# Householder reflections beside two attentions: three long steps each, or six short ones

## Chip, cores and metric

The kernel runs on one core of a Trainium2 chip. The metric is the device time of one execution in microseconds (us). "Before" is the kernel without the change, "after" the kernel with it. Engines are named as in the profile: PE is TensorE, DVE is VectorE, ACT is ScalarE, POOL is GpSimd, SP is SyncE, which here only issues DMAs.

## The reference

The activations x have the shape (4, 512, 288) and pass through four layers. L0 is an attention with adaptive layer norm and a mixture of four experts, of which two serve each token. L1 and L3 are attentions with adaptive layer norm and a dense two-layer MLP. L2 is a rotation in a 64-dimensional subspace that depends on a weight P (288 x 64) and on the condition, but not on x:

```python
U, _ = jnp.linalg.qr(P)                       # 288 x 64
R = _rotation(cond, W, b)                     # expm of a skew 64 x 64 matrix
z = jnp.einsum('btn,nd->btd', x, U)
z_rot = jnp.einsum('btd,bde->bte', z, R)
x_rot = x + jnp.einsum('btd,nd->btn', z_rot - z, U)
```

The attentions have 16 heads of 18 features and 512 positions for each of the four batches; all arithmetic is float32.

## The kernel before

**Order of the layers.** One program runs L0's attention (`attention(0, ...)`), the experts of L0, L1's attention, L1's MLP, the rotation's products, L3's attention and L3's MLP, one behind the other. Nearly all of the time belongs to matmuls on PE.

**The work that runs beside.** The subspace U of L2 depends on weights alone, so the kernel computes it beside the layers ahead of L2. `rotation()` (L839) is a Python generator: `reflections()` (L584) makes the QR of P by 64 Householder reflections, one after the other, on the transposed matrix `pT` (64 rows on partitions, 288 columns, and two more columns for the head and the factor of the reflection at hand). Then `subspace()` turns the reflections into U. Each `yield` ends a step. `tick()` (L863) advances the first generator of the list `beside` by one step, and the places where tick() is called decide between which other instructions a step's instructions are issued. At first the list holds only `rotation()`; in round 4 of L0's attention the rest of L0's modulation is put ahead of it for a short while (L1234), and L3's modulation is appended behind it.

**One reflection k, before the change, is three steps:**
- *The long step.* `reflect` (L572) applies reflection k - 1 to the rows that are left: `headed` (L553) copies the head (L554), `dots` (L557) multiplies rows and v and sums (L560, which the profile shows as a product and an accumulator read), L577 makes the factor `w2`, and L578 updates `pT`. Then the norm of the next row: `dots` again, `n2` (L611) and `sgn` (L612), all on DVE, and the square root as a power on POOL (`nrm`, L613).
- *The short step.* Six small DVE operations (L618 to L623: `sn`, head, `den`, its maximum, reciprocal, factor `c`), and then `reflector` (L546) issues on SP a DMA (L550) that spreads the row of `pT` over the partitions of the tile `v`.
- *An idle step*, in which nothing is issued, so that the DMA can land. In the experts' phase, where the flag `far` is set, there are two such steps.

The flag `inside` (L861) is true while an attention issues its quads. Two helpers fix the order within an engine: `beside_of("DVE", ...)` ties an instruction behind the last row maximum issued so far (`take`, L98), and the scheduler may move an instruction that is not tied as its data allow. In the long step the head's copy and the norm's dot are tied to that maximum, in the short step `sn` is.

**The attention.** There are 16 rounds, one for each batch and group of four heads. A round has eight *quads*, k = 0 to 7. A quad (L980) issues two score matmuls for the row maxima of round r and two transposed score matmuls of lagging work, alternating; each lands in a PSUM bank. DVE takes the row maximum of the first kind (`row_max`, L954, the reduction is L965), ACT the exponential of the second kind (`weight`, L967, L977). The four banks are few, so a quad's matmuls wait until the DVE maximum and the ACT exponential of the quads before have freed them. Behind each quad other work is issued (L1237 to L1245): queries and keys, values (their additions on DVE are L917), the sums with the probabilities (`sums`, L990), projections, layer norms. At the end of a round, behind quad 7, `shift` (L1005) turns the maxima over on PE and subtracts them on DVE (L1019), which the next round's lagging matmuls need; this is called the round's border below. Rounds begin with round 0 before the loop of L1230; its border is behind its last quad.

**Where the ticks stand.** In the loop over the quads, L1252 to L1254:

```python
some = ticks if r < feed.sorts_from else ticks // 2
if k % 2 and (k + 3) % (gaps // some) == 0:
    tick()
```

`gaps` is 8. L0's attention has ticks = 4, so a step stands behind quads 1, 3, 5 and 7; from round 10 on (`sorts_from` of the experts, whose sorting takes DVE time there) only behind quads 1 and 5. L1's attention has ticks = 2: behind quads 1 and 5 in all rounds. L3's attention has nothing left to run beside it. The last loop (L1259 to L1271) issues the lagging quads of the last round, with one tick in each place where `k % (NT // ticks)` is 0.

**Other users of SP's queue.** During L0's attention SP issues the copies of the experts' weights (`w1c`, L1586) and a few others, in program order with the DMAs of v.

Of the kernel before, what the change touches and what calls it, by code (L numbers as in the profile page):

```python
# [46 lines left out]
def kernel(ctx: ExitStack, tc: tile.TileContext, a: dict, out: bass.AP):  # L47
# [21 lines left out]
    def bank(tag, name):  # L69
        return psum.tile([P, 512], F32, tag=tag, name=name, bufs=banks[tag])  # L70
# [30 lines left out]
    def beside_of(engine, instruction):  # L101
        if engine in taken:
            ordered(instruction.ins, taken[engine])

    def in_turn(engine, instruction):

        beside_of(engine, instruction)
        take(engine, instruction)
# [427 lines left out]
    pT = cst.tile([RK, C + 2], F32, tag="pT", name="pT")  # L536
# [9 lines left out]
    def reflector(n, k):  # L546

        v = bgp.tile([RK, C + 2], F32, tag="v", name=f"{n}_{k}", bufs=4)
        r = RK - 1 - k
        nc.sync.dma_start(v[0:r, 0 : C + 2 - k], spread(pT[r : r + 1, k : C + 2], r))  # L550
        return v

    def headed(k, v, n):  # L553
        beside_of("DVE", nc.vector.tensor_copy(v[0:n, 0:1], v[0:n, C - k : C - k + 1]))  # L554
        return v[0:n, C - k + 1 : C - k + 2]

    def dots(k, m, v, n):  # L557
        junk = bgp.tile([RK, C], F32, tag="junk", name=f"junk_{k}", bufs=1)
        w = small.tile([RK, 1], F32, tag="w", name=f"w_{k}")
        ins = nc.vector.tensor_tensor_reduce(  # L560
            out=junk[0:n, 0 : m.shape[1]],
            in0=m,
            in1=v,
            scale=1.0,
            scalar=0.0,
            op0=ALU.mult,
            op1=ALU.add,
            accum_out=w[0:n],
        )
        return w[0:n], ins  # L570

    def reflect(k, m, v, n):  # L572

        c = headed(k, v, n)
        w, _ = dots(k, m[0:n, k:C], v[0:n, 0 : C - k], n)
        w2 = small.tile([RK, 1], F32, tag="w2", name=f"w2_{k}")
        nc.vector.scalar_tensor_tensor(w2[0:n], w, -1.0, c, ALU.mult, ALU.mult)  # L577
        nc.vector.scalar_tensor_tensor(  # L578
            m[0:n, k:C], v[0:n, 0 : C - k], w2[0:n], m[0:n, k:C], ALU.mult, ALU.add
        )  # L580
# [3 lines left out]
    def reflections():  # L584

        nc.gpsimd.memset(back, 0.0)
        nc.gpsimd.affine_select(
            out=back,
            in_=back,
            compare_op=ALU.not_equal,  # L590
            fill=1.0,
            base=1 - RK,
            pattern=[[1, RK]],
            channel_multiplier=1,
        )
        ps = bank("de", "psback")
        nc.tensor.matmul(ps[0:RK, 0:C], lhsT=back, rhs=pT[:, 0:C], start=True, stop=True)
        nc.vector.tensor_copy(pT[:, 0:C], ps[0:RK, 0:C])
        for k in range(RK):
            n = RK - k  # L600

            def one(name):
                return small.tile([RK, 1], F32, tag=name, name=f"{name}_{k}")[0:n]


            alpha, tail = pT[0:n, k : k + 1], pT[0:n, k + 1 : C]
            hd, c = pT[0:n, C : C + 1], pT[0:n, C + 1 : C + 2]
            n2, nrm, sgn = one("n2"), one("nrm"), one("sgn")
            rest, ins = dots(k, tail, tail, n)
            beside_of("DVE", ins)  # L610
            nc.vector.scalar_tensor_tensor(n2, alpha, alpha, rest, ALU.mult, ALU.add)  # L611
            nc.vector.tensor_scalar(sgn, alpha, 0.0, 2.0, ALU.is_ge, ALU.mult)  # L612
            in_turn("POOL", nc.gpsimd.tensor_tensor(nrm, n2, phalf[0:n], ALU.pow))  # L613
            yield


            sn, den, rden = one("sn"), one("den"), one("rden")
            beside_of("DVE", nc.vector.scalar_tensor_tensor(sn, sgn, -1.0, nrm, ALU.add, ALU.mult))  # L618
            nc.vector.tensor_add(hd, alpha, sn)
            nc.vector.tensor_mul(den, sn, hd)  # L620
            nc.vector.tensor_scalar_max(den, den, TINY)
            nc.vector.reciprocal(rden, den)
            nc.vector.scalar_tensor_tensor(c, rest, 0.0, rden, ALU.is_gt, ALU.mult)  # L623
            if n > 1:
                v = reflector("v", k)
                yield
                yield
                if far[0]:
                    yield
                reflect(k, pT, v, n - 1)  # L630

    def subspace():

# [205 lines left out]
    def rotation():  # L839
        yield from reflections()  # L840
        yield from subspace()
        for b in range(B):
            ps = bank("de", f"psue_{b}")
            for kc in range(KC):
                nc.tensor.matmul(
                    ps[0:CP, kc * RK : (kc + 1) * RK],
                    lhsT=uT[halves[b // HB], kc * CP : (kc + 1) * CP],
                    rhs=ef[halves[b // HB], b % HB, :],
                    start=True,
                    stop=True,  # L850
                )
            nc.vector.tensor_copy(
                ue[:, b, :, :],
                ps[0:CP, 0 : KC * RK].rearrange("p (k j) -> p k j", j=RK),
            )
            yield

    beside, aside = [rotation()], [exponential()]  # L860
    inside, far = [False], [False]  # L861

    def tick(works=beside):  # L863
        while works and next(works[0], works) is works:
            works.pop(0)


    def attention(l, w, mod, eps, feed, ticks, hT=None, then=None, also=()):

# [10 lines left out]
        with ExitStack() as es:  # L880
# [99 lines left out]
            def quad(halves):  # L980

                for k in range(2):
                    for what, r, n in halves:
                        t, i = n // 2, n % 2 * 2 + k
                        if what is row_max:
                            row_max(r, t, i)
                        else:
                            ps[r, t, i] = weight(r, t, i)
# [133 lines left out]
            def lagging(k):  # L1122

                return [(weight, k // (2 * NT), k % (2 * NT))] if k >= 0 and k < n * 2 * NT else []
# [59 lines left out]
            def work_off(jobs, pieces):  # L1184
                for one in pieces:
                    if one in jobs:
                        next(jobs[one], None)
# [22 lines left out]
            n, gaps = len(groups), 2 * NT  # L1210

            def started(jobs):

                for kind, job in jobs.items():
                    if kind != "R":
                        next(job)
# [13 lines left out]
            for r in range(1, n):  # L1230
                jobs, pieces, steps = others(r)
                started(jobs)
                if r == NG and then is not None:
                    beside.insert(0, then)  # L1234
                for k in range(gaps):
                    quad([(row_max, r, k)] + lagging(8 * r + k - 9))
                    for step in steps[k]:  # L1237
                        step()
                    if k == 1 and r > 1:
                        sums(r - 2, 2)  # L1240
                        sums(r - 2, 3)
                    if k == 5:
                        sums(r - 1, 0)
                        sums(r - 1, 1)
                    work_off(jobs, pieces.get(k, ""))  # L1245
                    if k == gaps - 1:
                        for kind, job in jobs.items():
                            if kind != "R":
                                drain(job)
                        shift(r)  # L1250

                    some = ticks if r < feed.sorts_from else ticks // 2  # L1252
                    if k % 2 and (k + 3) % (gaps // some) == 0:
                        tick()  # L1254

            jobs, _, steps = others(n)
            jobs["A"] = feed.activations()
            started(jobs)
            for k in range(NT + 1):  # L1259
                quad(lagging(8 * n + 2 * k - 9) + lagging(8 * n + 2 * k - 8))  # L1260
                if k < NT:
                    for step in steps[2 * k] + steps[2 * k + 1]:
                        step()
                work_off(jobs, feed.last_pieces[k])
                if k == 0:
                    sums(n - 2, 2)
                    sums(n - 2, 3)
                if k in (2, 3):
                    sums(n - 1, k - 2)
                if k < NT and k % (NT // ticks) == 0:  # L1270
                    tick()  # L1271
            inside[0] = False
            hidden = feed.first(places_of_first())
            next(hidden)
# [14 lines left out]
    def drain(work):  # L1289
        for _ in work:  # L1290
            pass
# [1023 lines left out]
    turning = rotate()  # L2315
# [114 lines left out]
```

## Time and profile before

| what | us |
|---|---|
| three timed executions | 1946.29, 1946.56, 1951.55 (median 1946.56) |
| the profiled execution, its own time | 1953.08 |
| its span, first to last instruction | 1951.4 |
| L0's attention, rounds 1 to 15 | about 47 to 400 of the span |
| L1's attention, rounds 1 to 15 | about 882 to 1204 |
| L3's attention, rounds 1 to 15 | about 1451 to 1769 |
| copies of v before the update (L554), first and last | 71.0 and 1311.2 |
| POOL's power (L613), 64 of them, busy | 35.9 |

In the rows of the profile a line gives the source line, engine, operation, output and inputs with their shapes and the count, then busy time and mean duration of one, then the idle time that the engine had just before these instructions, and what ended it ("<-PE a0s L79" is the matmul that filled tile a0s). Tiles of L0's, L1's and L3's attention begin with a0, a1 and a3; "m" is the tile of the maxima's scores, "s" that of the exponentials'. A matmul stands as two rows of the hardware, so the 256 maxima go with 512 matmul rows. In timelines the columns are start, duration, engine, line, operation, tiles and count, and in brackets the idle time ahead. PEclk gives the clock that PE was granted in 40 slices of the span.

### The profile page before, as it was taken

To read this page: it belongs to the slowest core of one execution; us is meant where nothing else is said; L and a number is where in the kernel's file an instruction comes from. 1 tells how busy PE (TensorE), PEld (TensorE's weight loads), DVE (VectorE), ACT (ScalarE), POOL (GpSimd) and SP (SyncE) were. 2 spreads that over 40 slices of the span, in tenths; PEclk is the share of its full clock that TensorE was granted. 3 is DMA by queue.
4 is the path that set the end of the run, shared out by engine and by line. 5 is a ranking of instruction groups with operands and counts; after the bars stand their busy time and mean duration, and the time that the engine had idled before them with its cause. 6 is when DMAs were issued, how large, how long until landed. Compare 5 with 4: busy or idle time off the path is not lost. (4 is left out here: it accounts for less than half of the span.)

```text
span 1951.4 us, 27946 instructions
## 1 busy us (share of the span) xinstructions
PE 1879.7 (96%) x10385; PEld 997.6 (51%) x10385; DVE 1014.7 (52%) x2836; ACT 740.8 (38%) x1375; POOL 542.9 (28%) x795
## 2 busy tenths in 40 slices
PE   7999999999999999999999999999999999999998
PEld 4434443446777677774344433555554444433565
DVE  4667777734423343447766667162355666564201
ACT  1544454443222122224555455231225555455220
POOL 3021321235344347622322123112401121212101
PEclk9989999889999999999999999999999999999999
DMA  7411122326686457621211111300000111111000
GB/s 148 100 36 39 20 57 54 85 56 195 173 238 201 144 178 221 199 85 31 45 32 28 30 32 19 76 9 5 22 1 14 36 37 23 28 27 23 18 16 25
DMA packets 86986, 136.91 MB, mean 70 GB/s; under 512 B 32292, under 2 KB 67663, under 8 KB 86851
## 3 DMA queue, kind: packets, MB, share of 16 engines
q1 hardware_dynamic: 63554, 61.46, 14.0%
q0 software_dynamic: 23184, 73.66, 12.9%
q8 instruction: 82, 1.34, 0.3%
q14 instruction: 54, 0.43, 0.1%
q10 hardware_dynamic: 112, 0.01, 0.0%
HBM read 103.25 MB, written 20.08 MB: 63 GB/s over the span
## 5 line engine op out<-in xcount | busy, mean ns | idle before, releaser
L965 DVE TENSOR_REDUCE max<-a3m 128x1 f32<-128x512 f32 x256 | 164.7, 686 | 126.5 <-PE a3s L79 117.5
L965 DVE TENSOR_REDUCE max<-a0m 128x1 f32<-128x512 f32 x256 | 165.2, 684 | 91.1 <-PE a0s L79 79.4
L965 DVE TENSOR_REDUCE max<-a1m 128x1 f32<-128x512 f32 x256 | 164.5, 684 | 90.7 <-PE a1s L79 84.6
L977 ACT ACTIVATE a0p<-a0s 128x512 f32<-128x512 f32 x256 | 141.1, 596 | 158.0 <-PE a0s L79 157.7
L977 ACT ACTIVATE a1p<-a1s 128x512 f32<-128x512 f32 x256 | 140.2, 596 | 138.8 <-PE a1s L79 138.8
L977 ACT ACTIVATE a3p<-a3s 128x512 f32<-128x512 f32 x256 | 140.0, 596 | 135.8 <-PE a3s L79 135.7
L79 PE MATMUL a0m<-a0qk,a0qk 32*128 32x512 f32 x512 | 167.0, 659 | 9.0 <-DVE max L965 7.8
L79 PE MATMUL e0h<-e0hT,e0w 128*128 128x256 f32 (+1 forms) x918 | 168.4, 393 | 1.6 <-ACT e0hT L2019 0.9
L79 PE MATMUL e0o<-e0w,e0hm 128*128 128x288 f32 x648 | 167.0, 411 | 2.0 <-ACT e0hT L2019 1.9
L79 PE MATMUL a0s<-a0qk,a0qk 32*128 32x512 f32 x512 | 168.3, 665 | 0.0
L79 PE MATMUL a1m<-a1qk,a1qk 32*128 32x512 f32 x512 | 151.9, 640 | 7.4 <-DVE max L965 6.2
L79 PE MATMUL a3m<-a3qk,a3qk 32*128 32x512 f32 x512 | 150.2, 640 | 6.8 <-DVE max L965 5.5
L613 POOL TENSOR_TENSOR nrm<-n,phalf 64x1 f32<-64x1 f32 (+31 forms) x64 | 35.9, 560 | 429.3 <-DVE n L611 429.1
L79 PE MATMUL a1s<-a1qk,a1qk 32*128 32x512 f32 x512 | 153.3, 639 | 0.2 <-DVE v L554 0.2
L79 PE MATMUL a3s<-a3qk,a3qk 32*128 32x512 f32 x512 | 151.6, 639 | 0.2 <-DVE a3qk L1019 0.2
L79 PEld LDWEIGHTS e0h<-e0hT,e0w 128*128 128x128 f32 (+1 forms) x918 | 128.5, 189 | 34.4 <-issue 14.6
L79 PEld LDWEIGHTS e0o<-e0w,e0hm 128*128 128x128 f32 x648 | 120.0, 190 | 37.0 <-ACT e0hT L2019 5.1
L1399 ACT ACTIVATE e0hm<-e0h,e0w 128x256 f32<-128x256 f32 x144 | 60.5, 470 | 124.5 <-PE e0h L79 123.4
L79 PEld LDWEIGHTS a0m<-a0qk,a0qk 32*128 32x128 f32 x512 | 49.2, 187 | 76.0 <-DVE max L965 41.9
L79 PE MATMUL f1h<-f1hT,w 128*128 128x512 f32 (+1 forms) x216 | 81.3, 616 | 0.4 <-ACT f1hT L509 0.4
L79 PE MATMUL f3h<-f3hT,w 128*128 128x512 f32 (+1 forms) x216 | 79.4, 613 | 0.4 <-ACT f3hT L509 0.4
L79 PEld LDWEIGHTS a1m<-a1qk,a1qk 32*128 32x128 f32 x512 | 44.3, 182 | 69.2 <-DVE max L965 48.4
(524 smaller groups left out, 3152.6 us busy)
## 6 DMA issues: line engine op xcount, KB each, us to landing
eo<-e0r SPq DMA_DIRECT2D x50, 144.0 KB
ada<-in_ada SPq DMA_DIRECT2D x18, 324.0 KB
wr<-in_wrot SPq DMA_DIRECT2D x16, 288.0 KB
xm<-e0m SPq DMA_DIRECT2D x6, 768.0 KB
g<-gates SPq DMA_DIRECT2D x24, 144.0 KB
w<-in_w SPq DMA_DIRECT2D x6, 432.0 KB
x<-in_x SPq DMA_DIRECT2D x16, 144.0 KB
w1c<-in_w SPq DMA_DIRECT2D x8, 288.0 KB
```

Of the source, the lines that this page charges most:

```text
L79: ins = nc.tensor.matmul(*args, **kwargs).ins
L613: in_turn("POOL", nc.gpsimd.tensor_tensor(nrm, n2, phalf[0:n], ALU.pow))
L965: take("DVE", nc.vector.tensor_reduce(m[:, t, i, D : D + 1], ps, AX.X, ALU.max))
L977: take("ACT", nc.scalar.activation(p, ps, AF.Exp, scale=D**-0.5))
L1399: nc.scalar.activation(self.hms[i][f], ps[r], func, bias=b1(f)),
```

## The change

Inside an attention a reflection becomes six steps, and the steps come twice as often. `reflect` becomes a generator with a `yield` ahead of the update of `pT`, and another follows behind the update, ahead of the norm of the next row; both hold only while `inside` is true. The idle steps become two there. In the six steps of a reflection are, in this order: the norm with POOL's power; the short step with the DMA of v; nothing; nothing; copy, dot and `w2` of the application; the update.

A new helper `tick_turning` gives a step to the rotation alone, when it is first in the list. In L0's attention it stands behind the even quads of rounds 1 to 9, so every quad has a step there; from round 10 on, and in L1's attention, it stands behind quads 3 and 7, so every second quad has one. In the last loop it follows every tick. L0's modulation, when it is ahead of the rotation, keeps its old places.

```diff
+    def between():
+        if inside[0]:
+            yield
+
     def reflect(k, m, v, n):
         c = headed(k, v, n)
         w, _ = dots(k, m[0:n, k:C], v[0:n, 0 : C - k], n)
         w2 = small.tile([RK, 1], F32, tag="w2", name=f"w2_{k}")
         nc.vector.scalar_tensor_tensor(w2[0:n], w, -1.0, c, ALU.mult, ALU.mult)
+        yield from between()
         nc.vector.scalar_tensor_tensor(
             m[0:n, k:C], v[0:n, 0 : C - k], w2[0:n], m[0:n, k:C], ALU.mult, ALU.add
         )
...
                 yield
                 yield
-                if far[0]:
+                if far[0] or inside[0]:
                     yield
-                reflect(k, pT, v, n - 1)
+                yield from reflect(k, pT, v, n - 1)
+                yield from between()
...
-    beside, aside = [rotation()], [exponential()]
+    turning = rotation()
+    beside, aside = [turning], [exponential()]
...
+    def tick_turning():
+        if beside and beside[0] is turning:
+            tick()
...
                     if k % 2 and (k + 3) % (gaps // some) == 0:
                         tick()
+                    elif (k + 3) % (gaps // some) == gaps // some // 2:
+                        tick_turning()
...
                 if k < NT and k % (NT // ticks) == 0:
                     tick()
+                    tick_turning()
             inside[0] = False
```

## Prediction

> **What bounds the kernel now.** First the page: busy times, the granted clock, the groups.
>
> ```profile
> PE 1879.7 (96%) x10385; PEld 997.6 (51%) x10385; DVE 1014.7 (52%) x2836; ACT 740.8 (38%) x1375; POOL 542.9 (28%) x795
> ...
> PEclk9989999889999999999999999999999999999999
> ...
> L79 PE MATMUL a0m<-a0qk,a0qk 32*128 32x512 f32 x512 | 167.0, 659 | 9.0 <-DVE max L965 7.8
> ...
> L79 PE MATMUL a1m<-a1qk,a1qk 32*128 32x512 f32 x512 | 151.9, 640 | 7.4 <-DVE max L965 6.2
> L79 PE MATMUL a3m<-a3qk,a3qk 32*128 32x512 f32 x512 | 150.2, 640 | 6.8 <-DVE max L965 5.5
> ```
>
> TensorE sets the end: 96% of the span. VectorE is half idle, so taking work off it is worth nothing by itself; what counts is where TensorE waits for VectorE. The score matmuls do: 9.0 us idle before them in L0's attention (a0), 7.4 in L1's (a1), 6.8 in L3's (a3). L3's attention holds no reflection, so it is the yardstick for what reflections cost.
>
> Idle time understates it: when the maxima come late, the four matmuls of a quad go out in two pairs, which the records count as busy. So I read the TensorE timeline from one quad's first matmul to the next one's, with half of any half-clock time taken off, and set each quad of a0 and a1 beside the same quad of a3 ("r.k" is round r, quad k). One example, the VectorE timeline and then the TensorE timeline:
>
> ```profile
> 102.36 1.29 DVE L965 TENSOR_REDUCE max<-a0m 128x1 f32<-128x512 f32 x2 [1.27 <-PE a0s L79]
> 103.57 0.14 DVE L554 COPY v<-v 61x1 f32<-61x1 f32 x1
> ...
> 104.42 0.51 DVE L578 SCALAR_TENSOR_TENSOR pT<-v,w,pT 61x286 f32<-61x286 f32 x1
> 104.96 0.45 DVE L560 CUSTOM_DVE_ANT_0 junk<-pT 61x284 f32<-61x284 f32 x1
> ...
> 105.45 0.21 DVE L611 SCALAR_TENSOR_TENSOR n<-pT,w 61x1 f32<-61x1 f32 x1
> 105.58 1.27 DVE L965 TENSOR_REDUCE max<-a0m 128x1 f32<-128x512 f32 x2
> ```
>
> ```profile
> 103.77 0.69 PE L79 MATMUL a0m<-a0qk,a0qk 32*128 32x512 f32 x1
> ...
> 106.31 0.69 PE L79 MATMUL a0m<-a0qk,a0qk 32*128 32x512 f32 x1 [0.78 <-DVE max L965]
> ```
>
> The long step runs 103.57 to 105.58, 2.01 us, while VectorE has only the 1.27 us shown ahead of the max at 102.36 to spare per quad. The next maxima start late, TensorE waits 0.78, and 3.4 takes 2.55 against 1.90 in a3: 0.65 lost. In all, for a0, rounds 2 to 10:
> - Long steps (2.0 to 2.2 us) at a round's border, where L917 and L1019 stand too (0.45 and 0.69 us on VectorE): quad 2.1 4.67 against 2.91, 7.1 4.53 against 2.91, 10.1 +1.25. Together 4.6.
> - Short steps (six operations, 1.07 us) at a border: 3.1 3.47 against 2.92, 8.1 4.05 against 2.91: 1.7.
> - Long steps elsewhere: 3.4 +0.65, 5.3 and 5.5 +0.56, 6.2 and 6.3 +0.82, 8.4 and 8.5 +0.63, 9.3 +0.20: 2.9.
>
> So some **9.2 us** in a0 are in reach; in a1, where steps are half as dense, **1.7** (4.3 +0.44, 8.6 and 8.7 +0.60, 10.2 and 10.3 +0.65). Later rounds of a0 differ from a3 by the experts' sorting too, and I claim nothing there.
>
> **The change part by part.** The pace is kept: a reflection takes six quads of a0 (twelve of a1) before and after, with the same instructions, so nothing is saved in busy time, and equally many reflections are done when each attention ends. The experts' phase, the end of the rotation and L3 see no edit.
>
> *The cut of the long step.* By the compiled order of the changed kernel the six steps are not six on VectorE: update (L578) and sign (L612) are moved up right behind copy, dot and w2, and only the next norm (dot and L611) stays a quad later. From the rows above, copy to sgn is 2.01 less the norm's 0.45 + 0.07 + 0.21 with its overlaps: about 1.45 to 1.55, then the norm 0.6 to 0.7, then the short step 1.07 as before. Where they now stand in a0:
> - The 1.5 us piece at or next to a border five times (3.6, 5.7, 8.7, 10.7, 13.7). A long one costs 1.25 to 1.76 there, mean 1.54; 0.6 shorter gives 0.95, bounds 0 and 1.54: 5 x 0.95 = 4.75.
> - It stands elsewhere seven more times where it could matter (1.4, 2.2, 3.0, 6.5, 7.3, 8.1, 9.5), 0.1 to 0.25 over the 1.27 to 1.4 to spare; bounds 0 and the 0.65 of 3.4; I take 0.1: 0.7.
> - A short step at a border once (1.7): 0.55 to 1.14, I take 0.85.
> - The norm piece at three borders (6.7, 9.7, 12.7): between 0 and the 0.55 of a step of 1.07 us, 0.2 each: 0.6.
>
> Together 6.9 against 9.2: **-2.3**. If no piece cost anything it would be -9.2; if each cost its upper bound, 7.7 + 4.55 + 1.14 + 1.65 = 15.0, +5.8.
>
> *The norm's power on POOL (L613).* It has one quad to finish instead of two. It takes 560 ns, and POOL waits for the norm 429.1 us over the kernel, so it is the one that waits: 0 in the rounds. In the last loop of a0 one power now stands behind four indirect loads of e0x (0.95 to 1.56 us each in POOL's timeline at 401 to 404): sn may wait up to some 3 us more. TensorE isn't bound by reflections there; I take 0, bounds 0 and 3.
>
> *The transfer of v (L550, on SP).* Issue to use shrinks from four quads to three in a0 (eight to six in a1), some 10 us to 7.5. One transfer has a full queue before it, the first:
>
> ```profile
> 56.96 5.73 SPq L1586 DMA_DIRECT2D w1c<-in_w  x9
> 62.73 0.59 SPq L1586 DMA_DIRECT2D w1c<-in_b  x1
> 63.65 2.29 SPq L1586 DMA_DIRECT2D w1c<-in_w  x2
> 66.04 0.88 SPq L550 DMA_DIRECT2D v<-pT  x1
> ```
>
> ```profile
> 59.86 1.29 DVE L965 TENSOR_REDUCE max<-a0m 128x1 f32<-128x512 f32 x2 [0.29 <-PE a0s L79]
> 62.43 1.29 DVE L965 TENSOR_REDUCE max<-a0m 128x1 f32<-128x512 f32 x2 [1.28 <-PE a0s L79]
> ...
> 70.95 0.15 DVE L554 COPY v<-v 63x1 f32<-63x1 f32 x1 [0.42 <-DMA v<-pT]
> ```
>
> Issued at 66.04 and used at 70.95, it took 4.9 us, and VectorE already waited 0.42 for it. In the compiled order of the change it moves from place 88 to 80 of SP's queue, between copies of w1c that issue every 0.6 us: 56.96 + 4 x 0.64 is about 59.5, landing near 64.4. But the copy of v now stands behind the max of 1.4, which ends at 61.15. VectorE is in order: behind that copy are the maxima of 1.5, due at 62.43. They would start at 64.4 + 1.5 = 65.9, 3.5 late; with 1.3 to spare TensorE loses about 2.2. Bounds 0 (lands in time, or the copies issue sooner) and 3.5; I take **+2.0**. Later transfers have little else in SP's queue during the rounds, and the a0 and a1 rows show no other wait for v.
>
> *L1's attention.* The 1.5 us pieces stand where long steps stood, so the 1.7 lost there falls by about 0.9. But the short step goes to a border in five of the rounds, where it never was. By 3.1 of a0 that is 0.55, by 8.1 1.14, by the 1.3 to spare nothing; I take 0.3 each, 1.4. Net **+0.5**, bounds -1.7 and +4.
>
> Sum: -2.3 + 2.0 + 0.5 = **+0.2 us**. The profiled execution took 1953.08 (span 1951.4), which makes 1953.3. The median shown is 1946.56, 6.52 below that execution; the three runs (1946.29, 1946.56, 1951.55) lie 5.2 apart. One half-clock stretch explains such a distance: in the profiled execution 114.28 to 124.52 ran at half clock, 10.24 us, which costs 5.1. I carry the distance over: 1953.3 - 6.5 = **1946.8**.
>
> *The clock.* The clock of that stretch fell after TensorE waits of only 0.78 (106.31), 0.76 (111.72) and 0.30 us (114.22) near each other, while waits of the same size elsewhere had no such end. So a new or a vanished stretch is worth 1.7 to 8.5 us either way (rows of 3.41, 6.83, 10.24 and 17.07 us of half clock). I take 0 and put it into the rivals. The Trainium skill's page "TensorE: Matmul & The Clock Gate", section "HAM oscillation — how this bites in real kernels", has the clock fall when a wait crosses a window of 3.4 us. By that rule no wait worked out here drops the clock, and the sum stays +0.2; by the row at 114.28 the shorter wait for v could, and it would be about +5.3. The row speaks against the change, the rule does not.
>
> **Rivals.**
> 1. *Smoothing works* (faster): every piece fits into VectorE's idle time and v lands in time. For it: idle of 1.27 before most maxima, and pieces of 0.65 and 1.07 fit. Against: the 1.5 piece doesn't, and nine of the pieces meet a border. Price: 11 in reach (9.2 + 1.7) less about 2 for the borders and 1 for v: -8, so 1938.6.
> 2. *The first transfer of v trips the clock* (slower): VectorE's wait of 3 us at 61 leaves TensorE idle for about 2 us, more than any wait before the stretch at 114.28, and a stretch of 10.24 us follows (+5.1). With the upper 3.5 for the wait itself: 0.2 + 1.5 + 5.1 = +6.8, so 1953.4. It decides once v lands later than about 62.5, when the spare 1.3 is used up.
> 3. *The change doesn't do what it says*: the step is cut, but a max that waits for 1.5 us loses as much as one that waits for 2.0, as update and sign stay with it. The -2.3 and the -0.9 go: +3.4, so 1950.0, within no change.
>
> **Chances.** What a measurement of this kernel can tell from no change is about 0.3%, 5.8 us, so 1940.7 to 1952.4 is "same". The forecast 0.37 (its own range 1942 to 1951), rival 3 0.15: same 0.52. Rival 1 0.20, rival 2 0.28. The range reaches part of the way into both: 1939.5 to 1955.0, which holds the bounds of the single costs as long as no two of them fall out at the same end.
>
> **What would show it.** Right: L578 directly behind L577 in every reflection, L611 behind other maxima; idle before a0m still 7 to 11 us; a wait of 2 to 3 us on "DMA v<-pT" near 61 and none later in a0; quads 7.1 and 10.1 shorter, 9.1 and 6.1 longer. Rival 1: a0m idle near a3m's 6.8, no wait for v. Rival 2: half clock soon after 61. It is wrong altogether if the experts' phase or the end of the rotation (before: last v used at 1311.2) moves, since I cost both at nothing.

## The result, and the profile after

The changed kernel takes 1963.36 us (median of 13 executions, 1957.2 to 1974.41), before 1954.53 (13 executions, the three shown earlier among them, 1946.29 to 1961.92). The ratio is 1.0044, with a 95% interval of 1.0024 to 1.0063: slower, by about 8.6 us, where no change was forecast and the range ended at 1955.0. The three executions of before that the prediction had (median 1946.56) lay at the low end of what this kernel does; so the ratio is the measure, not the distance from 1946.56.

The single executions of one kernel lie some 10 to 20 us apart, and most of that goes with the granted clock (the mean over an execution, as a share of full speed): over all executions here, within a kernel, 0.001 of mean clock goes with about 1.9 us. So beside each ratio I give a **difference at equal clock**: each execution's time moved with a slope of 1.88 us to a clock of 0.986, averaged, less the same for before on the same chip. Its standard errors are 0.4 to 1.0 us where nothing else is said, and one kernel that ran on two chips came out 1.9 us apart, so differences of 1 or 2 us decide nothing by themselves. Where an edit lowers the clock by its own waits, this measure leaves that part out. For the change it is +5.7 us; for the 13 executions of before that ran with it no clock is recorded, so before's value from four other chips stands in, 1954.5 to 1955.6. By this reckoning the remaining 3 us are the clock itself, 0.9839 on average against 0.9850 to 0.9865 of before on those chips.

The page after, in the lines that were shown of before:

```profile
PE 1882.7 (96%) x10385; PEld 1001.6 (51%) x10385; DVE 1010.7 (52%) x2836; ACT 740.4 (38%) x1375; POOL 543.6 (28%) x795
...
PEclk9999999989999999999999999999999899999999
...
L79 PE MATMUL a0m<-a0qk,a0qk 32*128 32x512 f32 x512 | 161.3, 645 | 10.5 <-DVE max L978 9.4
...
L79 PE MATMUL a1m<-a1qk,a1qk 32*128 32x512 f32 x512 | 155.2, 647 | 6.8 <-DVE max L978 5.5
L79 PE MATMUL a3m<-a3qk,a3qk 32*128 32x512 f32 x512 | 154.0, 655 | 6.8 <-DVE max L978 5.5
```

TensorE waits 10.5 us ahead of a0's score matmuls (before 9.0) and 6.8 ahead of a1's (before 7.4): the attentions changed by a few us in all. To see where the rest is, I cut the two profiled executions into stages and took half of the half-clock time out of each stage (all stage lengths below are such). L0's attention (rounds 1 to 15) is 3.8 us longer, the last loop behind it 1.1 shorter, the experts' phase, counted from its first matmul, 3.4 longer, L1's attention 0.1 shorter. The first figure leans on that correction: uncorrected, after's L0 attention is 6.4 us shorter, since before's has 27.3 us at half clock there and after's 6.8. **The experts' phase, where the change edits nothing, holds about as much of the loss as L0's attention.**

In L0's attention there is a wait for v that the prediction named, and one that it didn't. VectorE after:

```profile
59.98 1.29 DVE L978 TENSOR_REDUCE max<-a0m 128x1 f32<-128x512 f32 x2 [1.27 <-PE a0s L79]
62.68 0.14 DVE L554 COPY v<-v 63x1 f32<-63x1 f32 x1 [1.41 <-DMA v<-pT]
...
93.84 1.29 DVE L978 TENSOR_REDUCE max<-a0m 128x1 f32<-128x512 f32 x2 [0.30 <-PE a0s L79]
97.80 0.14 DVE L554 COPY v<-v 61x1 f32<-61x1 f32 x1 [2.68 <-DMA v<-pT]
...
99.27 1.27 DVE L978 TENSOR_REDUCE max<-a0m 128x1 f32<-128x512 f32 x2
```

TensorE and SP's queue behind the second of these waits:

```profile
100.00 0.69 PE L79 MATMUL a0m<-a0qk,a0qk 32*128 32x512 f32 x1 [1.79 <-DVE max L978]
```

```profile
58.02 0.89 SPq L550 DMA_DIRECT2D v<-pT  x1
...
86.94 0.70 SPq L1079 DMA_DIRECT2D a0or<-a0one  x1
87.69 0.45 SPq L532 DMA_DIRECT2D g<-gates  x1
88.25 2.33 SPq L550 DMA_DIRECT2D v<-pT  x1
```

The first v was issued at 58.02 and used at 62.68, 4.7 us later. The third was issued behind two other transfers (a0or and g, of 144 KB each in the view of transfers) and needed 9.5 us, 88.25 to 97.80; three quads are 7.5. That those two made it slow is argued; no run took them away.

In the experts' phase TensorE's longest waits for the matrix exponential, which runs beside the experts too, moved. First before, then after:

```profile
662.03 1.47 PE L793 MATMUL pss<-ef 64*64 64x64 f32 x16 [4.14 <-DVE ef L833]
712.61 1.04 PE L793 MATMUL pss<-ef 64*64 64x64 f32 x16 [1.97 <-DVE ef L833]
737.11 1.04 PE L793 MATMUL pss<-ef 64*64 64x64 f32 x16 [1.12 <-DVE ef L833]
```

```profile
610.29 0.68 PE L800 MATMUL pst<-m,nskew 64*64 64x64 f32 x8 [3.11 <-DVE m L824]
...
704.53 1.04 PE L800 MATMUL pss<-ef 64*64 64x64 f32 x16 [1.53 <-DVE ef L840]
735.56 1.47 PE L800 MATMUL pss<-ef 64*64 64x64 f32 x16 [7.66 <-DVE ef L840]
```

All its waits over 0.3 us there come to 7.8 us before and 13.7 after. What held VectorE ahead of the last one:

```profile
726.86 0.52 DVE L2088 SCALAR_TENSOR_TENSOR e0y<-e0y,two,g 128x288 f32<-128x288 f32 x1 [6.38 <-DMA e0y<-eo,place]
727.30 0.13 DVE L627 TENSOR_SCALAR den<-den 30x1 f32<-30x1 f32 x1
...
727.90 0.77 DVE L629 SCALAR_TENSOR_TENSOR pT<-w,rden 30x1 f32<-30x1 f32 x1
734.19 0.14 DVE L554 COPY v<-v 29x1 f32<-29x1 f32 x1 [5.51 <-DMA v<-pT]
...
735.00 0.87 DVE L840 SCALAR_TENSOR_TENSOR ef<-ef,pss 64x256 f32<-64x256 f32 x2
```

Read from above: a product of the experts' combination (L2088) stands in the middle of the short step and waits 6.38 us for a gather; so the factor (L629) comes late, v is issued late, its copy waits 5.51 us, and the exponential's `ef` stands behind that copy. In before the same short step stands whole, 0.91 us from its first start to its last, and the copy behind it waits less:

```profile
731.07 0.15 DVE L618 SCALAR_TENSOR_TENSOR sn<-sgn,nrm 30x1 f32<-30x1 f32 x1 [0.73 <-POOL nrm L613]
...
731.98 0.15 DVE L623 SCALAR_TENSOR_TENSOR pT<-w,rden 30x1 f32<-30x1 f32 x1
735.92 0.14 DVE L554 COPY v<-v 29x1 f32<-29x1 f32 x1 [3.80 <-DMA v<-pT]
```

In the compiled order the rotation now enters the experts' phase **one step ahead**: the changed kernel gave it twice as many steps (six for three), so where before had done one step of a reflection at the end of L0's attention, after has done two of six, the norm and also the short step. From there on 12 of the 29 transfers of v stand one to seven places earlier in SP's queue, spread over the whole phase.

### The profile page after: what moved, and what is told of

Its sections match the earlier page's. It is cut to its first block, busy times and chain, and to the rows that moved or that the text cites. A ratio compares the mean times of both kernels' runs of the same rounds, so it can differ in the third digit from the quotient of the medians.

```text
span 1961.6 us, 27947 instructions
## 1 busy us (share of the span) xinstructions
PE 1882.7 (96%) x10385; PEld 1001.6 (51%) x10385; DVE 1010.7 (52%) x2836; ACT 740.4 (38%) x1375; POOL 543.6 (28%) x795
## 5 line engine op out<-in xcount | busy, mean ns | idle before, releaser
L79 PE MATMUL a0m<-a0qk,a0qk 32*128 32x512 f32 x512 | 161.3, 645 | 10.5 <-DVE max L978 9.4
L79 PE MATMUL a0s<-a0qk,a0qk 32*128 32x512 f32 x512 | 162.4, 653 | 0.0
L2061 ACT COPY e0r<-e0o 128x288 f32<-128x288 f32 x38 | 15.1, 398 | 171.4 <-PE e0o L79 167.1
```

The lines of the kernel that those rows point to most:

```text
L79: ins = nc.tensor.matmul(*args, **kwargs).ins
L2061: take("ACT", nc.scalar.copy(y, ps))
```

## The experiments

Theory A put the loss into L0's attention (waits for v). Theory B put a third of it there and the rest down to half-clock time, drawn anew in each execution. Theory C put it into L1's attention. Theory D came with kernel 5: the shifted step in the experts' phase. Each kernel ran beside before on its chip. The difference at equal clock is called d.

**1. The change in L0's attention alone** (a flag limits `between`, the second idle step and `tick_turning` to it).

```diff
     def between():
-        if inside[0]:
+        if short[0]:
             yield
...
         inside[0] = True
+        short[0] = l == 0
```

> The six steps in L0's attention alone; in L1's attention the three steps as before. Theory A (the loss is made in L0's attention: the traces show VectorE waiting 1.41 and 2.68 us there for the DMA of v, which it waited 0.42 for before, and short steps meeting POOL's additions): slower than before by as much as the whole change, +6 to +10 us. Theory B (a third of the loss is stalls in L0's attention, the rest is half-clock time that is drawn anew in every execution): +3 to +4 us at an equal share of half clock, the rest by the draw, with a granted clock no lower than before's. Theory C (L1's attention or what follows it makes the loss): within 2 us of before.

Ratio 1.0042 (1.0019 to 1.0066), d +5.7: as much as the whole change. C falls, and so does B, which had 3 to 4 at equal clock.

**2. The change in L1's attention alone** (`short[0] = l == 1`).

> The six steps in L1's attention alone; in L0's the three steps as before. Theory A: within 2 us of before, since the quads of L1's attention lost and won the same (sum of the differences about 0). Theory B: the same. Theory C: +5 to +9 us.

Ratio 1.0021 (0.9993 to 1.0050), d +5.6. A and B missed; theory C had this number, but had already fallen with kernel 1. By the trace the change alone costs 6.3 us in L1's attention, and as part of the whole change nothing. The quads show where: here the 1.5 us piece (copy to update) falls behind quads 2.7, 5.7, 8.7, 11.7 and 14.7, at borders, and the quads 3.1, 6.1, 9.1, 12.1 take 0.76 to 0.79 more than before and 15.1 0.73; 15.5 takes 2.0 more. With both parts the same pieces fall behind quads 1 and 5. Which it is depends on the step with which the rotation enters L1's attention. So the cost of the whole is not the sum of the two parts.

**3. Both attentions, the application whole and late**, four quads for v.

```diff
         nc.vector.scalar_tensor_tensor(w2[0:n], w, -1.0, c, ALU.mult, ALU.mult)
-        yield from between()
...
-                yield from reflect(k, pT, v, n - 1)
+                yield from between()
+                reflect(k, pT, v, n - 1)
                 yield from between()
```

> All six steps in both attentions, but copy, dot, w2 and update stand together in the last of them, so that there are four quads (before: four; changed kernel: three) between the issue of v's DMA and its use in L0's attention; the norm still comes a quad later. Theory A: the waits for v in the first rounds fall from 1.41 and 2.68 us to under 0.5 each, and the time falls by 3 to 6 us below the changed kernel's, as the stalls and the half clock behind them go. Theory B: 2 to 3 us below the changed kernel's. Rival (the cut pieces at the rounds' borders cost the time, not the waits): within 1 us of the changed kernel's.

Ratio 1.0053 (1.0031 to 1.0075), d +8.3: slower than the change, against A and the rival alike. By stages: L0's attention 1.1 us *shorter* than before, 4.9 shorter than after, so with four quads for v that loss is gone, as A said; but L1's attention 5.2 longer (the pieces at borders, as in 2) and the experts' phase 5.1 longer.

**4. No reflections beside the attentions** (the changed kernel, whose steps inside an attention are empty).

```diff
             n = RK - k
+            if inside[0]:
+                for _ in range(6):
+                    yield
+                continue
```

> Leaves out the reflections that would fall into the two attentions (their steps are empty, so the experts' phase gets the same reflections at the same places). This is the yardstick for what all reflections beside attentions cost. From the quads of before beside those of L3's attention: 9 us in L0's and 2 us in L1's attention, so about 11 us below before, and 14 to 20 below the changed kernel, of which theory A puts the part above 15 down to half-clock time. If half-clock time is drawn whatever the reflections do (theory B), the granted clock stays as low as in the changed kernel.

Ratio 0.9913 (0.9881 to 0.9945), d -9.8: about what a better arrangement inside the attentions could win at most. L0's attention is 7.4 us shorter than before, L1's 2.6: the prediction's 9.2 and 1.7, read from single quads, were of the right size. The mean clock is 0.9876, not as low as the changed kernel's 0.9839, against theory B.

**5. Before, with one step more at the end of L0's attention.** Theory D alone.

```diff
                 if k < NT and k % (NT // ticks) == 0:
                     tick()
+                    if l == 0 and k == NT - 1:
+                        tick()
```

> Before with one step more in the last loop of L0's attention and nothing else: three long steps as before, but the rotation enters the experts' phase one step ahead, as it does in the changed kernel (whose transfers of v stand at the same places of SP's queue there). Theory D (part of the loss is this shift: at equal clock the experts' phase took 3.2 us more in the changed kernel, with VectorE waiting up to 9.0 us for v in front of the exponential's operations): +3 us at equal clock, all of it in the experts' phase. Rival (the shift is harmless, the traces differ there by chance): 0 within 1.

Ratio 1.0029 (1.0009 to 1.0048), d +4.9. One step more, with all long steps as they were, costs most of what the whole change costs, and by the trace all of it, 4.9 us, in the experts' phase. Much the same waits appear as after:

```profile
622.57 0.92 PE L793 MATMUL pst<-m,nskew 64*64 64x64 f32 x8 [3.55 <-DVE m L817]
...
748.68 1.47 PE L793 MATMUL pss<-ef 64*64 64x64 f32 x16 [7.23 <-DVE ef L833]
```

**6. The change in L0's attention alone, in step** (kernel 1 and in the last loop `if k < NT - 1: tick_turning()`).

> The six steps in L0's attention alone, less one step in the last loop, so that the experts' phase and L1's attention meet the rotation at the same steps as before. Theory D: the 5.5 us that the change in L0's attention alone cost at equal clock fall to the 3.8 of the quads in L0's attention, perhaps 2.5. Rival: still 5.5.

Ratio 0.9993 (0.9970 to 1.0016), d +1.9, where kernel 1 had +5.7. L0's attention is still 4.1 longer in the profiled execution, and the third v is still waited for:

```profile
100.94 0.15 DVE L554 COPY v<-v 61x1 f32<-61x1 f32 x1 [2.69 <-DMA v<-pT]
```

**7. Kernel 6 with the application whole and late** (as in 3).

> As the kernel above, and copy, dot, w2 and update together in the last of the six steps, so that v has four quads again in L0's attention. Theory D with the waits for v as the loss inside L0's attention: the 3.8 us there turn into -1, so within 2 us of before at equal clock. If the cut itself or other short steps make the loss, +3 as the kernel above.

Ratio 0.9978 (0.9959 to 0.9996), d -2.4. L0's attention is 1.3 shorter than before; VectorE's longest wait for v in its rounds is 0.21 us:

```profile
99.23 0.14 DVE L554 COPY v<-v 61x1 f32<-61x1 f32 x1 [0.21 <-DMA v<-pT]
```

This kernel has the lowest ratio of those with the full computation; kernel 8 can't be told from it.

**8. Kernel 7 with the long step cut in two**: copy, dot and `w2` in the last step, update and norm in the first of the next reflection, the update tied to its quad's maxima (the diff shows the tie).

```diff
-        nc.vector.scalar_tensor_tensor(
+        update = nc.vector.scalar_tensor_tensor(
             m[0:n, k:C], v[0:n, 0 : C - k], w2[0:n], m[0:n, k:C], ALU.mult, ALU.add
         )
+        if short[0]:
+            beside_of("DVE", update)
```

> As the kernel above, but the long step is really cut in two: copy, dot and w2 in the last step, update and norm in the first step of the next reflection, with the update tied behind its own quad's maxima so that it cannot move up. Four quads for v. Pieces of 0.8, 1.35 and 1.07 us, none over the spare time of a quad away from a border. If the pieces' length counts as the prediction had it, L0's attention takes 3 to 5 us less than before, and the whole kernel too at equal clock. If not, as the kernel above.

Ratio 0.9980 (0.9961 to 1.0000), d -1.1. L0's attention is 0.6 shorter than before, not 3 to 5: a miss. With v in time, the cut as such brings nothing that can be seen.

**9. The whole change with both entries repaired, and the true six pieces.** The first: one step less in the last loop of L0's attention, one more ahead of L1's rounds. The second: kernel 6 with the tie of kernel 8. They ran with 10 on a chip where before took 2018.23, some 60 us more; 36 to 37 of that is in the experts' phase by these two traces.

> The whole change, with only the meeting of the rotation with what follows repaired: one step less in the last loop of L0's attention, so that the experts' phase runs as in before, and one step more ahead of round 1 of L1's attention, so that L1's attention runs as in the changed kernel. Theory D (most of the loss is the rotation entering the experts' phase one step ahead, the rest is L0's attention): at equal clock 1 to 3 us above before, where the whole change cost 5.8. Rival (the six steps themselves cost the time): 5 to 6.

> Six steps in L0's attention alone, experts' phase in step with before, and the update tied behind its own quad's maxima, so that VectorE really has one short piece behind every quad: 0.8, 0.7, 0.65, 1.07 us and two empty. v has three quads. If the merged piece of 1.5 us was what kept the change from its gain (the prediction's third rival), L0's attention takes 2 us less than without the tie. If the waits for v decide, the same within 1 us.

The repaired whole change: 1.0032 (1.0012 to 1.0053), d +3.5, with L0's attention 4.0 longer. The true six pieces: 1.0010 (0.9991 to 1.0029), d -1.0, with L0's attention 0.2 shorter than in before's trace, although VectorE still waits 1.99 and 2.70 us for v. So where v has three quads, the merged piece cost L0's attention 4 us (2 against the trace of kernel 11's repaired change, which has the same attention); that it costs is what the prediction's third rival said. Why so much is argued, not shown: a wait for v holds the next maxima until the update too is done when it stands behind the copy, and less long when it doesn't.

**10. The exponential's products left out** (of the squarings, shown, and of the Taylor steps), without and with the extra step of 5.

```diff
         for k in range(NSQ):
-            ps = both(f"pss_{k}")
...
             yield
             yield
```

> Leaves out the Taylor steps and squarings of the exponential (its steps are empty), three long steps, experts' phase as in before. Yardstick for the next kernel. The waits of 4.1, 2.0 and 1.1 us of TensorE for the exponential's VectorE operations go, and the matmuls of the exponential with them: 10 to 25 us below before.

> The kernel above with one step more in the last loop of L0's attention. Theory D with the exponential as the link (VectorE waits for v, the exponential's operations stand behind it, TensorE waits for them): the 4.9 us at equal clock that the one step cost with the exponential fall to under 1. If the step costs through another way (SP's queue, POOL, the experts' own VectorE work), 3 to 5 us remain between this kernel and the one above.

Ratios to before 0.9725 and 0.9789, d between the two -1.8 with an error of 2.8: inconclusive on this chip. So on another one, with two more:

**11. The same pair, the repaired whole change again, and three steps ahead** (kernel 5 with a step more in the first three places: a whole reflection, so the same phase).

> Before with three steps more in the last loop of L0's attention, one in each of its first three places: a whole reflection more is done there, and the rotation enters the experts' phase in the same phase as in before, one reflection further on. If the phase decides: within 1.5 us of before at equal clock, with the waits of 4, 2 and 1 us for the exponential as in before. If being early decides (transfers of v pushed ahead of others in SP's queue): 5 us or more above before, as with one step.

Ratio 1.0006 (0.9986 to 1.0025), d -1.7. So it is the phase that counts, not the earliness. TensorE's longest waits stand where before's do, at 662.25, 712.92 and 737.43; the first is 7.36 us, longer than before's 4.14 (a miss in this part), the others are 1.68 and 1.14.

> The whole change with one step less in the last loop of L0's attention and one step more ahead of L1's rounds, once more, on a chip where the experts' phase is as short as in the first runs. Theory D: 2 to 4 us above before at equal clock, all of it in L0's attention; TensorE's waits for the exponential 4, 2 and 1 us as in before.

Ratio 1.0004 (0.9987 to 1.0022), d +1.6; L0's attention 2.0 longer in the profiled execution. By its ratio the repaired change can't be told from before here; the same kernel had 1.0032 and d +3.5 in 9, so both together leave some 2 us of the 5.7. TensorE's waits stand where before's do again:

```profile
661.55 1.48 PE L800 MATMUL pss<-ef 64*64 64x64 f32 x16 [5.03 <-DVE ef L840]
711.99 1.04 PE L800 MATMUL pss<-ef 64*64 64x64 f32 x16 [1.91 <-DVE ef L840]
737.19 1.04 PE L800 MATMUL pss<-ef 64*64 64x64 f32 x16 [1.82 <-DVE ef L840]
```

> Leaves out the Taylor steps and squarings of the exponential, three long steps, once more on another chip. Yardstick for the next kernel.

> The kernel above with one step more in the last loop of L0's attention. If the exponential links the step to TensorE: within 1.5 us of the kernel above at equal clock. If not: 3 us or more above it, as with the exponential.

Ratios to before 0.9879 (0.9855 to 0.9902) and 0.9912 (0.9889 to 0.9936); at equal clock the step costs 7.0 (error 1.0) without the exponential. So the exponential is not needed for the loss; without it something else waits in its place, here the turning of the experts' tokens:

```profile
748.91 0.69 PE L79 MATMUL e0xt<-ident,e0xs 128*128 128x128 f32 x2 [9.02 <-DVE gate L380]
```

In that kernel VectorE waits 8.87 us at 738.82 for a gather in the middle of a reflection's application, the norm comes late, and POOL, in order, holds the token gather (e0xs, 742.50) behind the power that waits for the norm (741.75).

**12. The threading taken away**: kernels 5 and 7 with the combination's products ordered behind the last operation of the short step before them, which `factor[0]` holds.

```diff
             def weighted(j):
...
+                if factor[0] is not None:
+                    ordered(ins.ins, factor[0])
                 in_turn("DVE", ins)
```

> Three long steps with one step more in the last loop of L0's attention, as in the kernel that cost 4.9 us at equal clock, and one order more on VectorE: the products of the experts' combination stand behind the last operation of the short step issued before them, so they no longer stand inside it. If the threading is the link: v's DMA issues some 8 us earlier at 740, TensorE's wait of 7.2 us there falls below 4 and the time by 2 to 5 us. If the link is another: as without the order, within 1 us.

Ratio 1.0016 (0.9993 to 1.0038), d +2.6, where kernel 5 on another chip had +4.9: 2.3 us back, with an error of 0.8. VectorE in kernel 5, then in this kernel:

```profile
732.89 0.14 DVE L618 SCALAR_TENSOR_TENSOR sn<-sgn,nrm 30x1 f32<-30x1 f32 x1
...
740.15 0.52 DVE L2074 SCALAR_TENSOR_TENSOR e0y<-e0y,two,g 128x288 f32<-128x288 f32 x1 [6.12 <-DMA e0y<-eo,place]
...
741.20 0.77 DVE L623 SCALAR_TENSOR_TENSOR pT<-w,rden 30x1 f32<-30x1 f32 x1
747.31 0.14 DVE L554 COPY v<-v 29x1 f32<-29x1 f32 x1 [5.34 <-DMA v<-pT]
```

```profile
728.06 0.14 DVE L618 SCALAR_TENSOR_TENSOR sn<-sgn,nrm 30x1 f32<-30x1 f32 x1
...
728.96 0.15 DVE L623 SCALAR_TENSOR_TENSOR pT<-w,rden 30x1 f32<-30x1 f32 x1
729.03 0.93 DVE L2077 SCALAR_TENSOR_TENSOR e0y<-e0y,two,g 128x288 f32<-128x288 f32 x2
...
734.02 0.14 DVE L554 COPY v<-v 29x1 f32<-29x1 f32 x1 [3.57 <-DMA v<-pT]
```

```profile
739.98 1.18 PE L795 MATMUL pss<-ef 64*64 64x64 f32 x16 [3.36 <-DVE ef L835]
```

The short step takes 0.9 us from first to last start, not 8.3, and TensorE's wait falls from 7.23 to 3.36, as expected. The wait near 618 stays, with 3.24 us (kernel 5: 3.55); where the rest of the loss comes from is not settled.

> The fastest version so far (six steps in L0's attention alone, application whole in the last step, v with four quads, experts' phase in phase with before) with the same order. There the short step is threaded with the combination too, but in fewer places: 0 to 3 us less than that version at equal clock.

Ratio 1.0007 (0.9982 to 1.0033), d -0.5 against -2.4 without the order: a miss. The order that helps one phase of the steps doesn't help the other. TensorE's three longest waits for the exponential there are 6.20, 3.51 and 3.51 us, against 5.59, 2.05 and 2.40 in kernel 7, so it may even hurt; the times alone, 1.9 us apart with an error of 1.1, don't settle that.

**The traces side by side.** Of the kernels with the full computation and no added order, off the chip of 9 and 10, four enter the experts' phase one step ahead (the changed kernel, 1, 3 and 5): their experts' phase is 3.4 to 5.1 us longer than before's, and TensorE waits 12.3 to 13.7 us there for the exponential. Seven enter in step (before, 2, 6, 7, 8 and both of 11 with the exponential): -1.2 to +1.6 us, and 7.4 to 10.6 us of waits. The two groups don't overlap. L0's attention, likewise: the five executions with the change's attention read 2.0 to 5.1 us longer than before's trace, the eight others with before's attention -0.1 to +1.9, and the four with four quads for v (3, 7, 8 and the second of 12) 0.6 to 1.3 shorter. So, from the middles of the groups, the change costs some 3 us in L0's attention and some 4 in the experts' phase; together that is a little more than its d of 5.7, within the scatter.

## Why the prediction was wrong, step by step

- **The failed step** is "equally many reflections are done when each attention ends. The experts' phase, the end of the rotation and L3 see no edit." The count is right to a reflection, but a reflection has steps, and after is one of them ahead. Kernel 5 measured the price of that alone: 4.9 us at equal clock, and a lower clock (0.9838 against 0.9850). The prediction put the experts' phase at nothing and said itself that it would be wrong altogether if it moved; no term of its sum bounded that. That rival 2's +6.8 comes near the measured +8.6 is luck: its cause, a half-clock stretch behind the first wait for v, didn't come.
- *The 1.5 us piece at a border*: predicted 0.95 each, 4.75 for five. Measured against before's quads, or a3's where before's had a cost of their own, quads 3.7, 6.1, 9.1, 11.1 and 14.1 took 0.63, 0.88, 0.85, 0.96 and 0.52 more: 3.8. Right in kind and nearly in size. That the update moves up was right, and kernel 9 shows that it mattered.
- *The first transfer of v*: predicted +2.0 by a wait of 3 us; it was issued 1.5 earlier than worked out, the wait was 1.41, and quads 1.5 and 1.6 behind it took 1.2 more. The mechanism was right, the size less than taken. But "later transfers have little else in SP's queue" was wrong for the third: 2.68 us of wait, and quads 3.1 and 3.2 took 1.9 more than before (3.1 alone 4.77 against 3.47). Kernel 7 shows that both waits go with four quads.
- *The short step* was put at 1.07 us everywhere. In 3.3 and 7.6 it stood beside POOL's additions and took over 2 us; 3.4 and 7.7 took 0.56 and 1.23 more than before. So L0's attention came to +3.8, not -0.3.
- *L1's attention*: predicted +0.5, measured -0.1. Kernel 2 shows that this hung on the step with which the rotation enters L1's attention, and could have been +6.
- *POOL's power at the end of a0*: sn waited 2.59 us, as bounded (up to 3); the last loop got 1.1 us shorter all the same, so nothing was lost by it that shows.
- *The clock*: held constant in the forecast; by the reckoning above it gave some 3 us. Rival 2 named a half-clock stretch behind the first wait for v: none follows it in the profiled execution, where the first stands at 375.58. Stretches of 6.83 and 10.24 us, from 611.10 and 730.56, stand where TensorE waited 3.11 and 7.66 us in the experts' phase. Three more, 17.1 us in all, stand in L3's attention, which holds no reflection: part of the clock's share is chance in any one execution. What the Trainium skill's page "TensorE: Matmul & The Clock Gate" (section "HAM oscillation — how this bites in real kernels") states, that the clock falls when a wait crosses a window of 3.4 us, fits the wait of 7.66 us. The stretch behind the wait of 3.11 us speaks for a shorter one being enough here.
- *The base*: the median of three executions was 8 us below the median of the 13.

## What to carry to other kernels

Work that is done in steps beside other work has a phase, and whoever changes the number of steps moves the phase of everything that follows; compare the compiled order through the end of the program, not up to the end of the edited stage. Look at what stands between the operations of a step that issues a transfer: one product in its middle that waits for somebody else's gather delayed the transfer by some 8 us here, and then all that stood behind its use. Keeping the step whole gave 2.3 us back in one phase of the steps and nothing in the other. Measure the parts in the phase that they will have: here two edits cost 5.7 and 5.6 us alone and 5.7 together, and the first of them, put back in step and with its transfer given the old four quads, came out 2.4 us below before (error 0.9).

## What the runs showed of the hardware that was not expected

Some small operations of VectorE were slower where POOL was adding. In the changed kernel three operations of the short step took 0.59, 0.71 and 0.72 us (0.15 elsewhere) beside POOL's additions:

```profile
105.51 0.59 DVE L624 SCALAR_TENSOR_TENSOR sn<-sgn,nrm 61x1 f32<-61x1 f32 x1
106.13 0.71 DVE L625 TENSOR_TENSOR pT<-pT,sn 61x1 f32<-61x1 f32 x1
106.88 0.72 DVE L626 TENSOR_TENSOR den<-sn,pT 61x1 f32<-61x1 f32 x1
```

```profile
104.54 3.05 POOL L1100 TENSOR_TENSOR x<-x,a0bg 128x288 f32<-128x288 f32 x4
```

That the additions are the cause is argued from their lying side by side; no run took them away, and in round 7 sn took 0.14 us beside such additions while the next two took 0.64 and 0.72. And one chip ran before some 60 us longer (2018.23 against 1952.72 to 1956.8 on four others), with the experts' phase 36 to 37 us longer in the traces of two kernels, half-clock time taken off. The two kernels without the exponential took only 31 and 33 us more there (1963.32 against 1932.23, 1972.7 against 1939.85). Why that chip does so was not tried.
